# Which loads stand ahead of a data-dependent branch: mask alone, or mask behind weights and tables

## The chip, the cores and the metric

The kernel runs on one core of one Trainium2 chip. The metric is the device time of one execution in microseconds (us). A profile is one execution of the same program, recorded by the hardware profiler; its times are counted from the start of its span.

## The reference, cut to what matters

Eight sequences of 512 tokens with 256 channels pass through four layers: attention with one shared key/value head, a null key and a bias table; attention over the 16 heads inside each token; a mixture of eight experts with a shared expert; and a transformer layer whose feed-forward part is again a mixture. The layers behind the first matter here only as the work that follows. In the first layer:

```python
sim = jnp.einsum('bhid,bjd->bhij', q, k)          # k has the null key in front of the 512 tokens
sim = sim + bias                                  # null bias, then attn_bias
sim = jnp.where(causal_mask, neg, sim)
...                                               # and the padding mask: which keys may be seen
```

The padding mask has 8 x 512 bytes. `True` marks a key that may be attended to, and the inputs are made so that this holds only for the last positions of a sequence: `lenS = 512 - randint(0, 129)`, `mask = not (position < lenS)`. So the first 384 positions of every sequence are `False`. The kernel doesn't take this for granted: it looks at the mask, and branches.

## The kernel before, in words

One function, `tile_adaln_attn_ffn`, writes instructions for five engines; a layer beneath it (Tile) allocates buffers, sets the semaphores and orders the instructions of each engine's queue. An engine executes its queue strictly in order. Loads are issued by the sequencers of SP and ACT (`nc.sync.dma_start`, `nc.scalar.dma_start`), in the order of their queues.

**Ahead of the branch** (lines 63 to 408) stand constants made on POOL, the tables `cst`, `wr` and `br_bc`, a fill of the token table in DRAM (`ids<-none`), and the weights of the first layer (`wq`, `wo`, each 1 MB, `wkv`, and the small `gin`, `nvcol`, `nk_bc`, `nv_bc`, `nb_bc`) and of the second (`load_oh`: `awq`, `awd`, `awup`, `awout`, `gout`, `bdown`, `bq`, `bup`, `bout`). The first 384 columns of the mask are loaded as two rows of 1536 bytes in one partition each (`early_keys`, lines 363 to 368); VectorE takes the maximum of each row and of both, and `kept` is 1 if any early key is set. VectorE also makes `wn`, the null key times the query weights (four products and four sums, lines 395 to 408).

**The branch** (lines 1111 to 1115): every engine reads `kept` from memory into a register and compares it. If it is set, `any_keys` runs, the general attention; with these inputs it is skipped. The skipping path holds, for each engine, an addition to its semaphores of what the skipped instructions would have counted, and for SP the same for the eight counters of the transfers, each after a wait until the transfers ahead of the branch have landed.

**Behind the branch** `late_keys` (line 812) always runs: attention for the last 128 queries against the last 128 keys, and for all earlier tokens a constant row (`row`, from the null value and `wo`). In order:

- loads of the shared expert (`wtT`, `wgT`, `gT`, `swg`, `swu`, `swd`, lines 1239 to 1245, written ahead of the call), of tokens (`xp`, two sequences each), of the mask's tail (`m8`) and of four pieces of `bias`;
- the null value: `nvb` on VectorE, eight matmuls `pn<-wo,nvb`, then `row`;
- `prepare` for each of four pairs of sequences: normalise `xp`, transpose (`pt_x`), scale on ScalarE (`xT`), keys (`pk`), queries (`pq`), values and null scores (`pv`);
- scores (`pss`), softmax, output, for 16 units, and beside them (`beside`) `rest_load` and `rest_add` for the tokens that take the constant row, the second layer (`one_over_heads`, whose products `pr` run on POOL), and the first parts of the expert layer.

Everything later (three more groups of experts, the transformer layer, its mixture) follows in the order in which the queues were written. Eight counters (semaphores) are shared by all transfers of SP and ACT, in turn: a transfer can be issued only when the one that had its counter before has landed.

Of the kernel before, what the change touches and what calls it, by code (L numbers as in the profile page):

```python
# [9 lines left out]
F32 = mybir.dt.float32  # L10
U8 = mybir.dt.uint8
# [29 lines left out]
def tile_adaln_attn_ffn(ctx: ExitStack, tc: tile.TileContext, a: dict, out: bass.AP):  # L41
# [30 lines left out]
    nc.sync.dma_start(cst, a["c_misc"])  # L72
# [19 lines left out]
    def rows_of(vec, n=P):  # L92

        return vec.partition_broadcast(n)
# [19 lines left out]
    with nc.allow_non_contiguous_dma(reason="narrow rows"):  # L114
        nc.sync.dma_start(w_chosen, a["w_route"].rearrange("(k p) n -> p k n", p=P))
    br_bc = mid.tile([P, 12], F32, name="br_bc", tag="br_bc")
    nc.scalar.dma_start(br_bc, rows_of(a["b_route"]))
# [77 lines left out]
    none = ohp.tile([P, places // P], I32, name="none", tag="prod", bufs=4)  # L195
    nc.gpsimd.memset(none, B * S)
    nc.sync.dma_start(ids_d.rearrange("(p n) o -> p (n o)", p=P), none)
# [8 lines left out]
    def oh_load(name, shape, src, eng=None):  # L206
        t = ohp.tile(shape, F32, name=name, tag=name)
        (eng or nc.sync).dma_start(t, src)
        return t

    def oh_wload(name, src, cols):
        n = src.shape[0] // P
        return oh_load(name, [P, n, cols], src.rearrange("(k p) n -> p k n", p=P))

    OH_STEPS = 29
    oh_w = {}

    def load_oh():
        with nc.allow_non_contiguous_dma(reason="small vectors by partition"):
            oh_w["gout"] = oh_load("gout", [P, KD], cols_of(a["g_out"]), nc.scalar)  # L220
            oh_w["bdown"] = oh_load("bdown", [64, 1], a["bdown"].unsqueeze(1), nc.scalar)
        oh_w["awq"] = oh_wload("awq", a["aWq"], D)
        oh_w["awd"] = oh_wload("awd", a["aWdown"], 64)
        oh_w["awup"] = oh_load("awup", [64, 512], a["aWup"])
        oh_w["awout"] = oh_wload("awout", a["aWout"], D)
        oh_w["bq"] = oh_load("bq_bc", [P, D], rows_of(a["bq"]), nc.scalar)
        oh_w["bup"] = oh_load("bup_bc", [P, 2 * D], rows_of(a["bup"]), nc.scalar)
        oh_w["bout"] = oh_load("bout_bc", [P, D], rows_of(a["bout"]), nc.scalar)
# [134 lines left out]
    kept_i = aw.tile([1, 3], I32, name="kept", tag="kept")  # L363
    for u in range(2):
        early_keys = ohp.tile([1, B // 2, LAST * P], U8, name="early_keys", tag="prod", bufs=4)
        nc.sync.dma_start(early_keys, a["mask"][u * (B // 2) : (u + 1) * (B // 2), 0 : LAST * P].unsqueeze(0))
        nc.vector.tensor_reduce(kept_i[:, u : u + 1], early_keys, AX.XY, ALU.max)
    nc.vector.tensor_tensor(kept_i[:, 2:3], kept_i[:, 0:1], kept_i[:, 1:2], ALU.max)

    def load(name, shape, src, eng=None):  # L370
        t = aw.tile(shape, F32, name=name, tag=name)
        (eng or nc.sync).dma_start(t, src)
        return t

    def wload(name, src, cols):
        n = src.shape[0] // P
        return load(name, [P, n, cols], src.rearrange("(k p) n -> p k n", p=P))

    with nc.allow_non_contiguous_dma(reason="small vectors by partition"):
        gin = load("gin", [P, KD], cols_of(a["g_in"]), nc.scalar)  # L380
        nvcol = aw.tile([P, 1], F32, name="nvcol", tag="nvcol")
        for j in range(2):
            nc.scalar.dma_start(nvcol[j * 64 : (j + 1) * 64, :], a["cond"][1].unsqueeze(1))
    wq = wload("wq", a["Wq"], H * DH)
    wo = wload("wo", a["Wo"], D)
    wkv = wload("wkv", a["Wkv"], 2 * DH)
    nk_bc = load("nk_bc", [P, DH], rows_of(a["cond"][0]), nc.scalar)
    nv_bc = load("nv_bc", [P, DH], rows_of(a["cond"][1]), nc.scalar)
    nb_bc = load("nb_bc", [P, H], rows_of(a["null_bias"]), nc.scalar)
    load_oh()  # L390
    bias_v = a["attn_bias"].rearrange("(g hh j) q k -> g j q hh k", g=2, hh=4, j=2)


    wn = aw.tile([P, KD, 2, 2, 4], F32, name="wn", tag="wn")
    for k in range(KD):
        for g in range(2):
            pr = ohp.tile([P, 8, DH], F32, name="wn_pr", tag="prod", bufs=4)
            nc.vector.tensor_tensor(
                pr,
                wq[:, k, g * 512 : (g + 1) * 512].rearrange("p (h d) -> p h d", h=8),  # L400
                bc(nk_bc, 1, 8),
                ALU.mult,
            )
            nc.vector.tensor_reduce(
                wn[:, k, g].rearrange("p j hh -> p hh j"),
                pr.rearrange("p (hh j) d -> p hh j d", j=2),
                AX.X,
                ALU.add,
            )
# [8 lines left out]
    def any_keys():  # L418
        fill()
# [392 lines left out]
    def late_keys(first_group):  # L812
# [3 lines left out]
        with ExitStack() as ph:  # L816
# [14 lines left out]
            load_x(0)  # L831
            load_x(1)
# [5 lines left out]
            for g in range(2):  # L838
                for j in range(2):
                    nc.sync.dma_start(bias[:, g, j], bias_v[g, j, tail, :, tail])  # L840
                    nc.gpsimd.affine_select(
                        out=bias[:, g, j],
                        in_=bias[:, g, j],
                        pattern=[[0, 4], [-1, P]],
                        compare_op=ALU.is_ge,
                        fill=MASKED,
                        base=0,
                        channel_multiplier=1,
                    )
            ones = wp.tile([1, P], F32, name="ones", tag="ones")  # L850
# [6 lines left out]


            nvb = wp.tile([P, P], F32, name="nvb", tag="nvb")
            nc.vector.tensor_copy(nvb, nvcol.to_broadcast([P, P]))  # L860
            pn = ps_m.tile([P, D], F32, name="pn", tag="m")
            for c in range(8):
                nc.tensor.matmul(pn, nvb, wo[:, c, :], start=(c == 0), stop=(c == 7))
            null_row = wp.tile([1, D], F32, name="null_row", tag="null_row")
            nc.scalar.copy(null_row, pn[0:1, :])
            mv, rs = ln_stats(wk, [pn])
            row = wp.tile([P, D], F32, name="row", tag="row")
            nc.vector.tensor_scalar(row, pn, mv[:, 0, 0:1], rs[:, 0:1], ALU.subtract, ALU.mult)
# [212 lines left out]
            for _ in range(6):  # L1081
                next(prep)

# [27 lines left out]
    kept = nc.values_load(kept_i[:, 2:3], min_val=0, max_val=1)  # L1111
# [110 lines left out]
    with ExitStack() as ph:  # L1222
# [16 lines left out]
        with nc.allow_non_contiguous_dma(reason="small vectors by partition"):  # L1239
            wtT = wload("wtT", a["wtT"], E)  # L1240
            wgT = load("wgT", [64, E], a["wgT"], nc.scalar)
            gT = load("gT", [64, B], a["condT"], nc.scalar)
        swg = wload("swg", a["sw_gate"], 2 * P)
        swu = wload("swu", a["sw_up"], 2 * P)
        swd = wload("swd", a["sw_down"], D)
# [263 lines left out]
        late_keys(chain(route(0), route(1), mixture(0), mixed(0)))  # L1509
# [558 lines left out]
```

## Time and profile before

| What | Value |
|---|---|
| Times of three runs | 1849.16, 1856.75, 1860.49 us (median 1856.75) |
| Time of the profiled execution | 1837.18 us |
| Its span | 1835.1 us |
| Busy, share of the span | PE 85%, DVE 56%, ACT 32%, POOL 31% |
| Chain that ended last | PE 54%, DVE 16%, issue 14%, POOL 8%, DMA 4% |
| Mean granted TensorE clock | 0.899 |
| Bytes moved | 157.77 MB, mean 86 GB/s |
| First PE instruction | 27.1 us |

PE is the TensorE matmul stream, PEld its weight loads, DVE is VectorE, ACT is ScalarE, POOL is GpSimd, SP is SyncE; SPq and ACTq are the sequencers that issue transfers. The time of the profiled execution is 2.1 us above its span. A busy share is a mean over stages with different limits: the question of this document lies in the first 60 us, where PE is idle at first.

### The profile page before, as it was taken

What the parts mean: (1) busy time and instruction counts of PE and PEld (TensorE: products, weight loads), DVE (VectorE), ACT (ScalarE), POOL (GpSimd) and SP (SyncE); (2) the same over time, 40 slices, a digit from 0 to 9 for tenths busy, and PEclk for the clock granted to TensorE, in tenths of its full rate; (3) what the DMA queues carried; (4) which work ended last, traced back from release to release, by engine and by line L of the source; (5) the groups of instructions that cost most, each with busy time, mean ns of one, the idle gap of its engine ahead of it and who ended that gap; (6) DMA issues with size and microseconds to landing.
All of it is one profiled execution on the core that took longest, in us unless ns stands there. A gap on an engine that the chain in (4) does not pass through costs nothing.

```text
span 1835.1 us, 23467 instructions
## 1 busy us (share of the span) xinstructions
PE 1568.9 (85%) x7720; PEld 880.9 (48%) x7720; DVE 1031.2 (56%) x2709; ACT 583.9 (32%) x1281; POOL 561.3 (31%) x534
## 2 busy tenths in 40 slices
PE   2897888789897999998999899899899899639995
PEld 1664656543433554443554344454433333228884
DVE  3877554356673655555545656545756656225566
ACT  0433323202222332332353332344343343203331
POOL 2444351425445433103001302201201001147775
PEclk9897788867777989998999998999999999959998
DMA  5121236701114531002850102462100000046872
GB/s 167 39 83 35 83 110 201 199 26 38 32 54 144 165 98 38 19 1 92 190 157 30 36 7 66 109 182 67 37 1 7 13 1 14 4 154 212 238 222 66
DMA packets 189460, 157.77 MB, mean 86 GB/s; under 512 B 43214, under 2 KB 173774, under 8 KB 189329
## 3 DMA queue, kind: packets, MB, share of 16 engines
q1 hardware_dynamic: 147520, 109.10, 20.7%
q0 software_dynamic: 13056, 29.67, 5.1%
q10 hardware_dynamic: 28752, 17.41, 3.2%
q8 instruction: 63, 1.03, 0.3%
q14 instruction: 69, 0.56, 0.1%
HBM read 117.00 MB, written 44.21 MB: 88 GB/s over the span
## 4 chain that ended last, share of the span: by engine, by line
PE 54%; DVE 16%; issue 14%; POOL 8%; DMA 4%; ACT 1%; SPq 0%; POOLq 0%; ACTq 0%; DVEq 0%
PE pss L1613 12%; PE po_s L1660 6%; PE pg L1433 5%; PE pq_s L1565 3%; DVE nmz L1615 3%; PE pk_s L1571 3%; POOL pr L321 3%; POOL xs L1387 3%; PE px_s L1700 2%; PE py L1446 2%; PE pst L1637 2%; PE prs L1689 1%; PE pg L1483 1%; PE pv_s L1592 1%; DMA w_gu<-in_w_up_dram 1%
## 5 line engine op out<-in xcount | busy, mean ns | idle before, releaser
L1615 DVE TENSOR_REDUCE nmz<-pss 128x1 f32<-128x512 f32 x512 | 334.3, 685 | 224.2 <-PE pst L1637 188.7
L1638 ACT ACTIVATE pT_s<-pst 128x512 f32<-128x512 f32 x512 | 282.1, 595 | 448.7 <-PE pst L1637 443.3
L1613 PE MATMUL pss<-k_s,q_s 32*128 32x512 f32 x1024 | 360.7, 682 | 42.9 <-DVE nmz L1615 42.9
L1637 PE MATMUL pst<-q_s,k_s 32*128 32x512 f32 x1024 | 339.6, 670 | 4.5 <-DVE nmz L1615 3.6
L1613 PEld LDWEIGHTS pss<-k_s,q_s 32*128 32x128 f32 x1024 | 103.9, 192 | 229.0 <-DVE nmz L1615 104.9
L1660 PE MATMUL po_s<-pT_s,v 128*32 128x512 f32 x1024 | 165.6, 633 | 8.0 <-ACT pT_s L1638 8.0
L1278 POOL DMA_INDIRECT yg<-y,slot x64 | 66.4, 1038 | 301.7 <-DMA y<-y 170.7
L321 POOL TENSOR_TENSOR pr<-qk 128x512 f32<-128x512 f32 x72 | 89.8, 1282 | 103.5 <-DVE qk L299 67.2
L1433 PEld LDWEIGHTS pg<-xT,w_gu 128*128 128x128 f32 x768 | 95.6, 201 | 40.4 <-ACT xT L1424 17.1
L1433 PE MATMUL pg<-xT,w_gu 128*128 128x128 f32 x768 | 102.7, 289 | 13.3 <-ACT xT L1424 6.9
L321 POOL TENSOR_TENSOR pr<-at,v_h 128x512 f32<-128x512 f32 x72 | 90.5, 1288 | 67.1 <-DVE at L336 38.9
L1637 PEld LDWEIGHTS pst<-q_s,k_s 32*128 32x128 f32 x1024 | 96.8, 190 | 19.6 <-DVE nmz L1615 9.5
L1387 POOL DMA_INDIRECT xs<-x,slot x64 | 63.4, 991 | 126.1 <-DVE slot L1379 108.0
L1888 PE MATMUL ph<-xTj,w 128*128 128x256 f32 x368 | 85.7, 387 | 0.0
L1211 POOL DMA_INDIRECT ids<-token_id,pi x32 | 31.7, 992 | 174.0 <-DVE pi L1208 157.8
L1902 PE MATMUL py<-w,h_e 128*128 128x256 f32 x368 | 83.5, 380 | 1.4 <-issue 1.4
L1891 ACT ACTIVATE h_e<-ph,b 128x256 f32<-128x256 f32 x92 | 43.5, 473 | 108.8 <-PE ph L1888 105.1
L1888 PEld LDWEIGHTS ph<-xTj,w 128*128 128x128 f32 x368 | 71.5, 195 | 10.3 <-ACT xTj L1876 0.2
L1438 DVE TENSOR_TENSOR hh<-hh,pg 128x256 f32<-128x256 f32 x48 | 20.2, 420 | 97.0 <-ACT hh L1437 97.0
L1902 PEld LDWEIGHTS py<-w,h_e 128*128 128x128 f32 x368 | 68.2, 190 | 10.1 <-issue 1.8
L1565 PE MATMUL pq_s<-yT,wqp 128*128 128x512 f32 x128 | 68.7, 663 | 0.9 <-DVE hh L1439 0.7
L1712 POOL TENSOR_TENSOR e_rs<-e_ve,mhalf 128x4 f32<-128x4 f32 x8 | 8.9, 1108 | 192.9 <-DVE e_ve L1710 192.7
(298 smaller groups left out, 2604.2 us busy)
## 6 DMA issues: line engine op xcount, KB each, us to landing
w<-in_w_dram SPq DMA_DIRECT2D x46, 512.0 KB
w_gu<-in_w_gate_dram SPq DMA_DIRECT2D x96, 128.0 KB
w_gu<-in_w_up_dram SPq DMA_DIRECT2D x96, 128.0 KB
w_dn<-in_w_down_dram SPq DMA_DIRECT2D x96, 128.0 KB
xg<-xs SPq DMA_DIRECT2D x48, 256.0 KB
y<-y ACTq DMA_DIRECT2D x48, 256.0 KB
rows<-xr SPq DMA_DIRECT2D x8, 544.0 KB
x<-x SPq DMA_DIRECT2D x8, 512.0 KB
```

The lines of the kernel that those rows point to most:

```text
L321: nc.gpsimd.tensor_tensor(pr, x, y, ALU.mult)
L1278: nc.gpsimd.indirect_dma_start(out=yg[t][:, c, :], out_offset=None, in_=y1_d[grp], in_offset=bass.IndirectOffsetOnAxis(ap=yi[:, c, t : t + ...
L1387: sc_ = nc.gpsimd.indirect_dma_start(out=xs_d, out_offset=bass.IndirectOffsetOnAxis(ap=slot[:, bl, c, t : t + 1], axis=0), in_=xb[:, t, :] ...
L1433: nc.tensor.matmul(pg[:, c, u, :], w[:, u, c, k, :], xT[:, k, u, :], start=(k == 0), stop=(k == KD - 1))
L1565: nc.tensor.matmul(pq, wqp[:, k, gs], yT[:, k, :], start=(k == 0), stop=(k == KD - 1))
L1613: nc.tensor.matmul(pss, qs[n][r, t * P : (t + 1) * P], ks[n][r, :], start=True, stop=True)
L1615: yield lambda: nc.vector.tensor_reduce(nmz[n % 2].rearrange("p t (h r) -> p t h r", h=4)[:, t, h, HD : HD + 1], pss, AX.X, ALU.max, negat ...
L1637: nc.tensor.matmul(pst, ks[n][r, c * P : (c + 1) * P], qs[n][r, :], start=True, stop=True)
L1638: yield lambda: nc.scalar.activation(pT[:, u, :], pst, AF.Exp)
L1660: nc.tensor.matmul(pos[n][hd * 32 : hd * 32 + 32, :], v_sets[b % 3][:, c, (4 * g + hd) * VW : (4 * g + hd) * VW + 32], ws[hd // 2][:, hd % ...
L1888: nc.tensor.matmul(ph_, w1[:, k, c * P : (c + 1) * P], xT[:, k, :], start=(k == 0), stop=(k == KD - 1))
L1902: nc.tensor.matmul(py[:, u, :], h[:, c, u * P : (u + 1) * P], w2[:, c, :], start=(c == 0), stop=(c == 3))
```

## The change

Ahead of the branch only the mask's first 384 columns are read by name, now with one sequence to each of eight partitions; a maximum on VectorE, a 1 x 1 matmul that adds the eight, and a minimum with 1 give `kept`. The loads of weights and tables become functions that are called inside `late_keys` (and, for the first two layers' weights, inside `any_keys`): after the first tokens the weights `wkv`, `wq`, `wo`, then the second tokens, the bias, the second layer's weights, the shared expert's, the tables. `wn` and the null value are made between the steps of the first `prepare`.

```diff
-    nc.sync.dma_start(cst, a["c_misc"])
...
-        nc.sync.dma_start(w_chosen, a["w_route"].rearrange("(k p) n -> p k n", p=P))
-    nc.scalar.dma_start(br_bc, rows_of(a["b_route"]))
...
-    none = ohp.tile([P, places // P], I32, name="none", tag="prod", bufs=4)
-    nc.gpsimd.memset(none, B * S)
-    nc.sync.dma_start(ids_d.rearrange("(p n) o -> p (n o)", p=P), none)
...
+    def tables():
+        ...
+        nc.scalar.dma_start(br_bc, rows_of(a["b_route"]))
+        nc.sync.dma_start(cst, a["c_misc"])
+        none = ohp.tile([P, places // P], I32, name="none", tag="prod", bufs=4)
+        nc.gpsimd.memset(none, B * S)
+        nc.sync.dma_start(ids_d.rearrange("(p n) o -> p (n o)", p=P), none)
...
-    kept_i = aw.tile([1, 3], I32, name="kept", tag="kept")
-    for u in range(2):
-        early_keys = ohp.tile([1, B // 2, LAST * P], U8, name="early_keys", tag="prod", bufs=4)
-        nc.sync.dma_start(early_keys, a["mask"][u * (B // 2) : (u + 1) * (B // 2), 0 : LAST * P].unsqueeze(0))
-        nc.vector.tensor_reduce(kept_i[:, u : u + 1], early_keys, AX.XY, ALU.max)
-    nc.vector.tensor_tensor(kept_i[:, 2:3], kept_i[:, 0:1], kept_i[:, 1:2], ALU.max)
+    early = ohp.tile([B, LAST * P], U8, name="early_keys", tag="prod", bufs=4)
+    nc.sync.dma_start(early, a["mask"][:, 0 : LAST * P])
+    some = ohp.tile([B, 2], F32, name="some", tag="hm")
+    nc.vector.memset(some[:, 1:2], 1.0)
+    nc.vector.tensor_reduce(some[:, 0:1], early, AX.X, ALU.max)
+    kept_i = aw.tile([1, 1], I32, name="kept", tag="kept")
+    with tc.tile_pool(name="k_ps", bufs=1, space=PSUM) as kp:
+        pn = kp.tile([1, 1], F32, name="batches", tag="batches")
+        nc.tensor.matmul(pn, some[:, 0:1], some[:, 1:2], start=True, stop=True)
+        nc.vector.tensor_scalar(kept_i, pn, 1.0, None, ALU.min)
...
+    def load_weights():
+        with nc.allow_non_contiguous_dma(reason="small vectors by partition"):
+            nc.scalar.dma_start(gin, cols_of(a["g_in"]))
+            nc.scalar.dma_start(nk_bc, rows_of(a["cond"][0]))
+            for j in range(2):
+                nc.scalar.dma_start(nvcol[j * 64 : (j + 1) * 64, :], a["cond"][1].unsqueeze(1))
+        nc.sync.dma_start(wkv, a["Wkv"].rearrange("(k p) n -> p k n", p=P))
+        nc.sync.dma_start(wq, a["Wq"].rearrange("(k p) n -> p k n", p=P))
+        nc.sync.dma_start(wo, a["Wo"].rearrange("(k p) n -> p k n", p=P))
+        nc.scalar.dma_start(nv_bc, rows_of(a["cond"][1]))
+        nc.scalar.dma_start(nb_bc, rows_of(a["null_bias"]))
...
     def any_keys():
-        fill()
+        load_weights()
+        null_scores()
+        load_oh()
...
             load_x(0)
+            load_weights()
             load_x(1)
...
+            load_oh()
+            load_rest()
+            tables()
...
-            for _ in range(6):
+            for k in range(6):
                 next(prep)
+                if k == 0:
+                    null_scores()
+                elif k == 3:
+                    null_value()
```

`null_scores` holds the eight instructions for `wn`, `null_value` those for `pn` and `row`, `load_rest` the loads of the shared expert. Their instructions and their sizes are those of before; the buffers are now allocated ahead of the branch.

## The prediction

> **What bounds the kernel now.** I read the page first: TensorE (PE) is busy for 85% of the span, and the chain that ended last is 54% PE. So most of the run is a queue of matmuls, and a change in the loads counts only where that queue stands still. The timeline of the first 60 us shows where it does (start, length, engine, line, operation; in brackets the idle time before and what ended it):
>
> ```profile
> 15.85 3.40 DVE L367 TENSOR_REDUCE kept<-early_keys 1x1 int32<-1x1536 uint8 x2 [5.86 <-DMA early_keys<-in_mask_dram]
> 19.78 0.14 DVE L368 TENSOR_TENSOR kept<-kept 1x1 int32<-1x1 int32 x1
> 24.69 0.20 POOL L851 MEMSET ones<- 1x128 f32 x1 [21.88 <-PEq L1112]
> 26.19 0.38 SPq L1232 DMA_DIRECT2D wtT<-in_wtT_dram  x1
> 26.27 0.58 DVE L860 COPY nvb<-nvcol 128x128 f32<-128x128 f32 x1 [3.24 <-DVEq L1112]
> 39.77 1.22 PE L921 MATMUL pt_x<-ident,xp 128*128 128x128 f32 x4 [7.48 <-DMA xi<-in_x_dram]
> 48.63 0.63 PEld L968 LDWEIGHTS pv<-wkv,xT 128*128 128x128 f32 x4
> 57.16 6.17 POOL L321 TENSOR_TENSOR pr<-qk 128x512 f32<-128x512 f32 x5 [10.50 <-DVE qk L299]
> ```
>
> The branch's number is ready at 19.92 (19.78 + 0.14), and nothing of the attention is issued until 26.19, which I call B. Tokens come after that: the first transpose is at B + 13.6, the first value matmul `pv` at B + 22.4, the first products `pr` on POOL at B + 31.0. Why the number is late is told by the waits of SP's queue (who waited for what: total, times, longest):
>
> ```profile
> SPq L372 <- DMA nvcol<-in_cond_dram: 5.2, 1, 5.2
> SPq L1111 <- DVE kept L368: 3.4, 1, 3.4
> SPq L1112 <- SPq L1112: 2.8, 1, 2.8
> SPq L208 <- DMA wo<-in_Wo_dram: 2.0, 1, 2.0
> SPq L1232 <- DVEq L1112: 1.9, 1, 1.9
> ```
>
> The mask stands behind `wo`, and `wo` could only be issued when `nvcol`, which had its counter before, had landed. The last two L1112/L1232 rows are the branch itself: 2.8 us of jump, then 1.9 us until VectorE, which had `wn` to finish (until 23.03), had jumped too. Last the table of stretches (length, busy time and instructions of PE, PEld, DVE, ACT, POOL; clock, DMA share, GB/s):
>
> ```profile
> 0.00:20.00 20.00, 0.00 (x0) 0.00 (x0) 5.59 (x8) 0.00 (x0) 2.15 (x16) 1.00 0.69 193
> 26.00:41.00 15.00, 6.40 (x20) 4.72 (x20) 5.53 (x19) 1.65 (x2) 7.02 (x10) 0.87 0.75 229
> ```
>
> 3.9 MB move ahead of the branch and 3.4 MB behind it, in two bouts with a gap; tokens are in the second.
>
> **The change, part by part.**
>
> *The number.* The mask is now SP's first transfer, at 0.80. Nearest row: `gT`, a small load after a quiet stretch, was issued at 26.73 and used at 30.00, 3.3 us later. The first bytes of the whole run flow about 1.2 us after the first issue. Bounds 2.0 to 4.1 for the landing; I take 3.5. The maximum over 384 columns: 1.74 us for 1536 (3.40 / 2), so 0.44. The 1 x 1 matmul has no row; the narrowest, `pv` with 16 columns, are 0.57 for four, and with two hand-overs I give it 0.5. The minimum costs 0.14 as L368. Sum 4.6 (3.1 to 5.3).
>
> *The branch.* From 19.92 POOL needed 4.8 to its first instruction (24.69), SP 6.3 with the wait for VectorE in it. VectorE has nothing queued behind the number now, so I take 4.8: the new B, called S, is 4.6 + 4.8 = 9.4, 16.8 sooner (bounds 3.1 + 3.2, VectorE's own jump, and 5.3 + 6.3: 6.3 to 11.6). In the built program `wr`, `cst` and `br_bc` are still issued ahead of the branch, behind the mask, and SP's skipping path waits for them; their 150 KB should land before 8, under the jump: nothing. Only `none` and its write to `ids` go behind it; POOL's fill took 0.34 among memsets that nobody awaits.
>
> *The loads behind it.* SP's order is now `xp`, `wkv`, `wq`, `wo`, `xp`, four `bias`, the second layer's weights, the shared expert's, `ids`, `xp`, two `x_rest`, two `xi`; ACT's is `gin`, `nk_bc`, `nvcol` twice, `nv_bc`, `nb_bc`, `m8`, `gout`, `bdown`, `bq`, `bup`, `bout`, `wgT`, `gT`, and only then the table load and `xT`. Counters are still eight in turn, and the program's waits show whom each follows:
> - `wq`: ACT's `bq` followed it before and went at 8.13, so it took 5.9 after its issue ended (2.25). Now it has 384 KB ahead, 1.3 at 290 GB/s: S + 1.3 + 5.9 + 1.3 = S + 8.5.
> - `wo` follows the first `nvcol` (5.75 from issue at 1.71 to 7.46): S + 1.1 + 5.75 = S + 6.9, and lands 5.6 later (7.46 to 13.10, where `awq` could follow it): S + 12.5.
> - ACT: `bq` follows `wq`; five issues of 0.45 and the table load of 1.28 are ahead of `xT`, which was 7 us idle before: S + 8.5 + 2.3 + 1.3 = S + 12.1. No cost beside `wo`, but it is as late.
> - VectorE: `wn` was hidden ahead of the branch. It now waits for `wq`, 4 x (0.67 + 0.67) = 5.4, to S + 13.9, with `gb` (0.22, waiting for `gT`, ACT's last) and the key copy `kT` queued behind it.
>
> *PE.* Its queue is `pt_x`, one `pn`, `pk`, `pn`, half of `pq`, six `pn`, the rest of `pq`, `pv`. The first `pn` waits for `wo`, S + 12.5, and holds `pk` behind it. Then 0.65 + 1.97 (`pk`) and a 0.6 copy on VectorE that frees the bank: `pq` at S + 15.7, against B + 17.3. From there 5.5 (`pq`) and 3.9 (six of eight `pn`, 5.2 before) give S + 25.1. The 0.5 clock at 37 to 47 us lay under `pk` and `pq` before (0.34 each, against 0.26 at 54); it rose 7.1 us after PE restarted at 39.8, which here falls at S + 19.6 and saves 1.0 or so on the rest: `pv` at S + 24.1. That is 1.7 later after the branch than before, so the null value, hidden under the wait for tokens until now, costs part of the lead: 16.8 - 1.7 = 15.1 us.
>
> [...]
>
> *Transfers as a whole.* `pr` on POOL stands behind the two `xi` additions, and those behind the last transfer of the list: 7.2 MB from S. At the 290 GB/s of the fullest stretches that takes 25 us and 2 to start: S + 27, hidden, for `qk` is due at S + 32.6. At 229 (the row of 26 to 41, start included) it is S + 31.5, and with the additions (1.5), `ln_rs` (0.7), a scaling (0.4) and `qk` (0.4), 3.0 together, `pr` starts at S + 34.5: 1.9 late. At 193 (the row of 0 to 20) S + 37.4 and 7.8 late. I take 229, as the list is of that kind, and charge 1.1, since the scores of the other units go on beside POOL: 14.0 us gained. From `pr` on, all five queues stand in the order of before, with the same counters.
>
> *Sum.* 1837.2 (the profiled execution, span 1835.1 and 2.1 around it) - 14.0 = 1823.2. The runs shown have the median 1856.75, 19.5 above that execution; the edit touches nothing that differs between them, so I forecast 1842.5 as a median.
>
> **Rivals.**
>
> [...]
>
> *The transfers eat the lead:* at 193 GB/s, 15.1 - 7.8 = 7 gained, 1849.5. For it: in the first 20 us the waits on counters held the mean to 193, and the list has the same narrow loads (`nvcol`, `gin`) in its counters. Against: 37 transfers are eight deep, and most are 128 KB or more.
>
> *The branch isn't sooner,* or the engines wait for something that the number didn't gate: then S stays above 20 and the gain is under 5, 1852 to 1857. The 3.4 us that SP idled for the number speak against it.
>
> *Slower:* the counters make a chain. 37 transfers over 8 are 4.6 rounds; `xi` then lands at 4.6 times the round. At the longest landing seen, 5.75, that is S + 27. It decides from 9.7 us a round: S + 44.8, `pr` at 57.2, no gain; at 13.8 a round it costs 19 us, 1876. Nothing shows a round above 5.75, but loads of 4-byte elements queued behind 0.5 MB of broadcast rows weren't seen either.
>
> **How the numbers follow.** Forecast (gain of 9 to 17) 0.58; more 0.20; transfers or branch take most of it 0.15; slower 0.07. One per cent, about what a measurement of this kernel can tell from no change, is 18.6 us: the forecast lies inside it, and the runs of before spread over 11 us, so a part of the first two cases shows as faster by over 1%: 0.32. Within it 0.60, slower 0.08. The range goes from 1828 (18 gained, 1839, and the 11 of spread below it) to 1856 (7 gained, 1850, and half the spread above it); the forecast's own is 1834 to 1850.
>
> **What would show it.** Right: SP's first issue behind the branch near 9.4 (6 to 12), `wo` the last thing that PE waits for before `pk`, `pv` near 33.5, `pr` near 43, and the same distances as before from there on. Wrong: an S above 13; PE waiting on `gT` through VectorE, or on the key copy; `pr` waiting long for `xi`; or a lead of 14 us at 60 us that is gone at 400, which would make a later wait on a transfer the bound.

## The result and the profile after

The changed kernel takes 1844.4 us (median of 8 runs, 1839.55 to 1856.69) against 1855.26 for the kernel before on the same chip (8 runs, 1848.73 to 1860.49). The ratio is 0.9948, 95% interval 0.9923 to 0.9972: 9.6 us less, between 5.2 and 14.3. In two further groups of runs, both on one chip, the same program came to 0.9930 (0.9903 to 0.9958) and 0.9943 (0.9920 to 0.9966) of the kernel before. So the gain is about 11 us, inside the forecast's 9 to 17 and below its 14.0.

The profiled execution of the changed kernel took 1843.17 us, span 1841.5: longer than the one profiled execution of before (1837.18), which lay below every one of its eight timed runs. Single spans of this kernel vary by more than the change is worth; what can be compared between profiles is the first 60 us, and even there one execution does not stand for all (experiment 5). Timeline of the kernel after (start, length, engine, line, operation; in brackets idle time and what ended it):

```profile
3.14 0.15 DVE L377 TENSOR_SCALAR kept<-batches 1x1 int32<-1x1 f32 x1 [0.28 <-PE batches L376]
8.46 0.39 SPq L846 DMA_DIRECT2D xp<-in_x_dram  x1
10.36 0.40 SPq L404 DMA_DIRECT2D wq<-in_Wq_dram  x1
10.37 1.20 ACTq L402 DMA_DIRECT2D nvcol<-in_cond_dram  x2
18.88 0.33 ACTq L233 DMA_DIRECT2D bq_w<-in_bq_dram  x1
19.08 0.37 SPq L405 DMA_DIRECT2D wo<-in_Wo_dram  x1
19.28 0.23 DVE L885 COPY nvb<-nvcol 128x128 f32<-128x128 f32 x1 [6.06 <-DMA nvcol<-in_cond_dram]
20.09 1.09 PE L944 MATMUL pt_x<-ident,xp 128*128 128x128 f32 x4 [16.98 <-DVE xp L937]
27.59 0.50 PEld L888 LDWEIGHTS pn<-wo,nvb 128*128 128x128 f32 x2 [6.81 <-DMA wo<-in_Wo_dram]
28.74 1.97 PE L954 MATMUL pk<-xT,wkv 128*64 128x256 f32 x4
31.65 2.64 PE L970 MATMUL pq<-xT,wq 128*128 128x256 f32 x8
36.73 1.89 PE L970 MATMUL pq<-xT,wq 128*128 128x256 f32 x8
38.45 0.55 PE L991 MATMUL pv<-wkv,xT 128*128 128x64 f32 x4
47.37 6.27 POOL L326 TENSOR_TENSOR pr<-qk 128x512 f32<-128x512 f32 x5 [1.02 <-DVE qk L304]
```

The number is ready at 3.29, the end of the first row (19.92 before); SP's first issue behind the branch is at 8.46 (26.19 before). Of these 17.7 us, 10.4 are left at the first `pv` (38.45 against 48.85) and 9.8 at the first `pr` (47.37 against 57.16). The rest is lost between 11 and 27.6 us, where PE does four transposes and nothing else. What SP waited for in the first 60 us (who for what: total, times, longest):

```profile
SPq L405 <- DMA nvcol<-in_cond_dram: 8.3, 1, 8.3
SPq L858 <- DMA wo<-in_Wo_dram: 6.5, 1, 6.5
SPq L1139 <- SPq L1139: 3.5, 1, 3.5
SPq L1138 <- DVE kept L377: 1.1, 1, 1.1
```

The old wait for `nvcol` (5.2 before) is back, at 8.3, ahead of the same `wo`. PE waits for that `wo` at 27.59 (the weight load of `pn`, `PEld`), with `pk` and all that follows behind it. The 1.1 and 3.5 are the number and the jump. In the table of stretches the DMA engines between 9 and 20 us moved 140 GB/s and were busy for half of the time; behind `wo`'s issue they filled up (columns: length, busy time of PE, PEld, DVE, ACT, POOL; clock, DMA share, GB/s):

```profile
9.00:20.00 11.00, 0.00 (x0) 0.00 (x0) 2.12 (x8) 0.00 (x0) 4.76 (x6) 1.00 0.50 140
20.00:30.00 10.00, 3.50 (x9) 1.97 (x10) 5.93 (x11) 2.12 (x3) 0.64 (x1) 1.00 0.79 239
```

### The profile page after: what moved, and what is told of

The parts are those of the page before. It is cut to its first block, busy times and chain, and to the rows that moved or that the text cites. A ratio compares the mean times of both kernels' runs of the same rounds, so it can differ in the third digit from the quotient of the medians.

```text
span 1841.5 us, 23475 instructions
## 1 busy us (share of the span) xinstructions
PE 1576.4 (86%) x7722; PEld 884.6 (48%) x7722; DVE 1023.5 (56%) x2709; ACT 584.5 (32%) x1281; POOL 561.7 (31%) x534
## 4 chain that ended last, share of the span: by engine, by line
PE 68%; DVE 14%; issue 6%; POOL 5%; DMA 3%; another core or an unknown queue 1%; ACT 1%; ACTq 0%; SPq 0%; POOLq 0%; DVEq 0%
PE pss L1646 15%; PE po_s L1693 7%; PE pg L1466 5%; PE ph L1921 4%; PE pq_s L1598 4%; DVE nmz L1648 3%; PE py L1935 3%; PE pk_s L1604 3%; PE px_s L1733 3%; POOL pr L326 3%; PE pst L1670 2%; PE py L1479 2%; PE pv_s L1625 2%; PE pg L1516 2%; PE pu L1523 1%
## 5 line engine op out<-in xcount | busy, mean ns | idle before, releaser
L1646 PE MATMUL pss<-k_s,q_s 32*128 32x512 f32 x1024 | 367.8, 690 | 65.9 <-DVE nmz L1648 62.7
L1670 PE MATMUL pst<-q_s,k_s 32*128 32x512 f32 x1024 | 347.5, 681 | 5.8 <-DVE nmz L1648 3.6
L1466 PE MATMUL pg<-xT,w_gu 128*128 128x128 f32 x768 | 100.4, 285 | 10.7 <-ACT xT L1457 6.8
L1921 PEld LDWEIGHTS ph<-xTj,w 128*128 128x128 f32 x368 | 71.6, 195 | 10.4 <-ACT xTj L1909 0.2
L1935 PEld LDWEIGHTS py<-w,h_e 128*128 128x128 f32 x368 | 68.2, 190 | 10.1 <-issue 1.7
```

The costliest lines, as they stand in the source:

```text
L1466: nc.tensor.matmul(pg[:, c, u, :], w[:, u, c, k, :], xT[:, k, u, :], start=(k == 0), stop=(k == KD - 1))
L1646: nc.tensor.matmul(pss, qs[n][r, t * P : (t + 1) * P], ks[n][r, :], start=True, stop=True)
L1670: nc.tensor.matmul(pst, ks[n][r, c * P : (c + 1) * P], qs[n][r, :], start=True, stop=True)
L1921: nc.tensor.matmul(ph_, w1[:, k, c * P : (c + 1) * P], xT[:, k, :], start=(k == 0), stop=(k == KD - 1))
L1935: nc.tensor.matmul(py[:, u, :], h[:, c, u * P : (u + 1) * P], w2[:, c, :], start=(c == 0), stop=(c == 3))
```

## The experiments

"Gain" is always 1 - ratio times the median of the kernel before on the same chip, with its interval. "Lead" is how much sooner the first `pr` starts than in the kernel before (57.16).

**1. Is it the wait on `nvcol`?** The two `nvcol` loads alone go ahead of the branch (called kernel 1 below).

```diff
+    with nc.allow_non_contiguous_dma(reason="small vectors by partition"):
+        for j in range(2):
+            nc.scalar.dma_start(nvcol[j * 64 : (j + 1) * 64, :], a["cond"][1].unsqueeze(1))
+
     def load_weights():
...
-            for j in range(2):
-                nc.scalar.dma_start(nvcol[j * 64 : (j + 1) * 64, :], a["cond"][1].unsqueeze(1))
```

> Only the two `nvcol` loads (64 x 4 bytes each) move from behind the branch to ahead of it, on ACT's queue; `wo` then follows `nv_bc` on its counter. In the changed kernel `nvcol` was issued at 10.4 to 11.6 and landed 8.3 later with the DMA engines nearly empty, SP waited 8.3 for it, `wo` was issued at 19.1 and landed at 27.5, and the first `pn` with `pk` behind it began at 27.6. Theory A (the counter and the narrow load hold `wo`, and `wo` holds PE): `wo` is issued at 14 to 16, lands at 22 to 24, `pk` begins at 24 to 25 and `pv` at 34 to 35 instead of 38.2; the time falls by 3 to 4 us. Rival B (the DMA engines' throughput sets when `wo` lands): `wo` is issued sooner but still lands at 26 to 28, `pv` at 37 to 38, time the same within 1.5 us. Rival C (VectorE sets the start: `gb` waits for `gT`, the last of ACT's loads, and the key copy stands behind it): `wo` lands sooner, `pk` too, but `pq` waits for the key copy, and `pv` gains under 2 us.

Measured: 1818.01 us, ratio 0.9942 (0.9920 to 0.9964), gain 10.6 (6.6 to 14.6). Its timeline:

```profile
16.45 0.37 SPq L407 DMA_DIRECT2D wo<-in_Wo_dram  x1
22.37 1.97 PE L956 MATMUL pk<-xT,wkv 128*64 128x256 f32 x4 [1.73 <-ACT xT L952]
24.26 2.71 PEld L890 LDWEIGHTS pn<-wo,nvb 128*128 128x128 f32 x10 [0.76 <-DMA wo<-in_Wo_dram]
31.96 0.55 PE L993 MATMUL pv<-wkv,xT 128*128 128x64 f32 x4
40.64 5.04 POOL L326 TENSOR_TENSOR pr<-qk 128x512 f32<-128x512 f32 x4 [1.01 <-DVE qk L304]
```

`wo` landed by 24.3 instead of 27.6, and `pv` came 6.5 sooner than in the profile after. The DMA engines, nearly empty by the expectation, were busy for half of the time in the profile after (0.50 between 9 and 20 us). In these two executions the landing speaks against B (throughput), which wanted `wo` at 26 to 28, and against C, which wanted under 2 us at `pv`. It is not the last word: a second execution of this kernel (experiment 5) had `wo` issued at 18.22, landed at 26.19, and `pv` at 36.19. The time gained hardly more than the changed kernel's 9.6, and not the 3 to 4 us more that A wanted. Two questions followed: does the lead count, and is 38.45 typical of the changed kernel?

**2. Is it `pn` on PE?** No load is moved; the null value is written after the whole first `prepare`.

```diff
-                elif k == 3:
+                elif k == 5:
                     null_value()
```

> The null value (`nvb`, eight `pn`, `row`) is written after the last step of the first `prepare` instead of after its fourth, so on PE `pk`, `pq` and `pv` stand ahead of `pn` and don't wait for `wo`. No load is moved. Theory A (PE was held by `pn`'s wait for `wo`): `pk` begins when `xT` is ready, near 24 instead of 28.7, and `pv` at 30 to 32 instead of 38.2; the eight `pn` (about 5 us) come behind it, so `row` is as late as before or 1 us sooner, the scores `pss` begin at 36 to 37 instead of 40.2, and the time falls by 2 to 4 us. Rival C (VectorE's `wn`, `gb` waiting for `gT` at 27.6, and the key copy behind them set the start): `pk` is early but `pq` waits until the key copy is done at 28 to 29, `pv` at 34 to 35. Rival D (`row` and not the scores is what the following work waits for): `pv` is 6 us sooner and the products `pr` are not (47.4 within 1), and the time is the same within 1.5 us.

Measured: 1820.17 us, ratio 0.9964 (0.9938 to 0.9990), gain 6.6 (1.8 to 11.3).

```profile
20.83 1.97 PE L954 MATMUL pk<-xT,wkv 128*64 128x256 f32 x4 [2.46 <-ACT xT L950]
29.91 0.55 PE L991 MATMUL pv<-wkv,xT 128*128 128x64 f32 x4
31.61 3.70 PE L888 MATMUL pn<-wo,nvb 128*128 128x256 f32 x16
37.51 0.54 DVE L891 TENSOR_SCALAR row<-pn,ln_mv,ln_rs 128x256 f32<-128x256 f32 x1 [0.47 <-POOL ln_rs L88]
```

`pk` and `pv` left the wait for `wo` behind, as A said, and `pv` was the earliest of all; C's 34 to 35 is out. But `row`, at 37.51, was only 1.7 sooner than in the profile after (39.20), and `pr` began at 45.2: the second layer starts from `row`. The time did not fall by A's 2 to 4 us, and whether the null value is better early or late is not shown: 6.6 lies below the changed kernel's gains, but the intervals overlap. D's mechanism is there; its size is not settled, because `wo` itself was issued at 13.7 here and not at 19.1.

**3. Which half of the change brings the gain?** The first layer's loads are put back ahead of the branch, behind the mask, with the new way to form the number (weights ahead); in a second kernel the loads of `load_oh` and `tables` too (all ahead).

```diff
+    load_weights()
     def null_scores():
...
             load_x(0)
-            load_weights()
             load_x(1)
```

> The loads of the first layer's weights (`wkv`, `wq`, `wo` and the narrow `gin`, `nk_bc`, `nvcol`, `nv_bc`, `nb_bc`) are issued ahead of the branch again, behind the mask; everything else stays as in the changed kernel. Theory A (what counts is when `wo` lands, and the DMA engines were empty from 0 to 9 us): `wo` is issued near 8, lands at 14 to 15, and SP's part of the branch, which waits for all transfers ahead, ends at 15 to 17; tokens land 3.5 to 5 us behind that, the first transpose is at 20 to 22, nothing waits for `wo` any more, `pv` is at 31 to 33, and the time is 4 to 6 us below the changed kernel. Rival E (only an early first issue behind the branch counts, as the kernel's change supposes): the first issue is 7 to 8 later than 8.4 and `pv` is later than 38.2 by some of that, so the time is 2 to 6 us above the changed kernel.

> All loads of weights and tables stand ahead of the branch as in the kernel before, but behind the mask, and the new way to form `kept` is kept. This splits the change in two: the mask's place and form alone, without the loads behind the branch. Theory F (before, the number gated the branch, 19.9; the landings would gate it only a little sooner): SP can't leave the branch until the loads ahead of it have landed, so its first issue is at 17 to 20 against 26.2 before and 8.4 after, and `pv`, with all weights there, 22 us behind it or less: 38 to 42 against 48.6 and 38.2. The time is 6 to 11 us below the kernel before, so the mask's place brings most of the gain and the place of the loads little or nothing. Rival G (the loads' place brings the gain): first issue at 23 or later, `pv` at 45 or later, time within 4 us of the kernel before.

Measured: weights ahead 1822.7 us, ratio 0.9955 (0.9930 to 0.9981), gain 8.2 (3.5 to 12.8), first issue behind the branch at 15.90, lead 9.1. All ahead: 1829.16 us, ratio 0.9993 (0.9974 to 1.0012), gain 1.3 (-2.2 to 4.8), first issue at 24.56, lead 4.6. With all loads ahead the number was ready at 3.31, and still VectorE left the branch at 24.4 and SP at 24.6: the landings gate it as firmly as the number did (SP issued the last load ahead at 19.57, after a wait of 4.6 for `wo`). F's 17 to 20 is refuted, and so is its claim that the mask's place brings most of the gain; G's time holds, though not its `pv` at 45 (43.3). Moving the mask without the loads is worth 1.3 us, and 4.8 at most by its interval.

With the weights ahead, A missed in the time (8.2 gained is not 4 to 6 more than the changed kernel's 9.6) and E in the mechanism (`pv` at 36.7, not behind 38.2, though experiment 5 has the changed kernel's `pv` at 32.45 too): `wo` had landed before the branch, but `pt_x` came only at 26.56 instead of 20 to 22. The timeline shows a queue that nobody had on the list:

```profile
18.98 0.43 DVE L83 BATCH_NORM_STATS2 ln_st<-xp 128x6 f32<-128x256 f32 x1 [1.28 <-DMA xp<-in_x_dram]
24.53 0.64 POOL L859 TENSOR_SCALAR_AFFINE_SELECT bias<-bias 128x512 f32<-128x512 f32 x1 [2.80 <-DMA wgT<-in_wgT_dram]
25.13 0.72 POOL L88 TENSOR_TENSOR ln_rs<-ln_ve,mhalf 128x2 f32<-128x2 f32 x1
26.56 1.09 PE L944 MATMUL pt_x<-ident,xp 128*128 128x128 f32 x4 [23.47 <-DVE xp L937]
```

The tokens were there at 18.98, and `ln_rs` stood on POOL behind a piece of `bias` that had waited 2.80 (the row puts this wait down to the landing of `wgT`). When the landings come in another order, an engine's queue, which was written for the old one, can find a new instruction to stand behind.

**4. Does a microsecond of the branch count? And how steady is a profile?** Three kernels on one chip: the changed one and the one before, unchanged; and the changed one with 16 useless sums on VectorE, on which the number waits.

```diff
-    some = ohp.tile([B, 2], F32, name="some", tag="hm")
...
+    some = ohp.tile([P, 9], F32, name="some", tag="hm")
+    spin = ohp.tile([P, 8, DH], F32, name="spin", tag="prod", bufs=4)
+    nc.vector.memset(spin, 1.0 / DH)
+    for _ in range(16):
+        nc.vector.tensor_reduce(some[:, 1:9], spin, AX.X, ALU.add)
...
-        nc.tensor.matmul(pn, some[:, 0:1], some[:, 1:2], start=True, stop=True)
+        nc.tensor.matmul(pn, some[0:B, 0:1], some[0:B, 1:2], start=True, stop=True)
```

> The changed kernel once more, unchanged, on the chip of this group, so that the others can be set against it and not only against the kernel before. In the first group the gain in time was some 4 to 5 us smaller than the lead of the first products `pr` in each kernel (lead 16.6, 12.0, 9.1, 4.6; gain 11 to 12, 6.6 to 9, 6 to 8, 0 to 1). Theory H (something behind the front takes a fixed 4 to 5 us from every kernel with the loads or the mask moved): with `pr` at 47 (lead 9.8) the gain here is 4 to 6 us. Rival I (a lead counts in full, and the first group's kernels differ from their leads by the clock's chance only): 9 to 11 us.

> The kernel before, unchanged, for a second profile, on the chip of this group. Theory J (when TensorE's clock is halved follows from the work and comes again in every execution): the stretches at half clock lie at the same places of the span as in the first profile (10.2 us of them at 47.7, 20.5 at 153.5, 20.5 at 215), and the distances from `pr` to the first `xg` transpose (226 us) and on to the end are the same within 3 us. Rival K (they fall by chance): they lie elsewhere, and the distance from `pr` to `xg` differs by more than 5 us.

> The changed kernel with 16 useless sums of 512 columns on VectorE (0.68 us each in this case's profiles, some 11 to 12 us together) ahead of the branch's number; the number, the branch and all loads behind it are the same, only later. Theory M (a microsecond of the branch is a microsecond of the end): the number is ready at 12.5 to 14 instead of 3.3, the first issue behind the branch is at 17.5 to 19 instead of 8.4, all that follows keeps its distances, and the time rises by 9 to 11 us against the changed kernel on the same chip, to that of the kernel before. Rival N (later stages give back or take a part of any lead): the front moves as much, but the time by less than 6 us.

Measured: after 1823.54 us, ratio 0.9930, gain 12.8 (7.7 to 17.8), lead 10.6. Before again: 1832.65, ratio 0.9997 (0.9972 to 1.0022). The late number: 1832.78, ratio 0.9991 (0.9973 to 1.0009), gain 1.7 (-1.7 to 5.0); number at 13.79, first issue at 18.81, 10.35 later, and 9.2 us longer than the changed kernel on the same chip. M's 9 to 11 holds for the time: the two ratios' intervals don't overlap (0.9973 against 0.9958), so the delay costs time, though they don't exclude N's less than 6. H's gain of 4 to 6 us is refuted for the changed kernel.

But in the late kernel `pr` was only 4.3 later than in the profile after, although everything started 10.35 later: in that execution `wo` was issued 5.9 behind the first issue, not 10.6. So the front isn't the same in every execution, and M's "all that follows keeps its distances" failed. Theory J, that the clock's halvings come again at the same places, held only in part (the expectation counts its places 10.7 us later than from the start of the span, which is used here). By the clock's records the second profile of before has the 10.2 us at 36.7 (37.0 in the first) and 20.5 at 204.0 (204.2), but 23.9 at 139.1 instead of 20.5 at 142.8, and 20.5 at 227.8 where the first had 3.4 at 238.4 and 6.8 at 248.6; from `pr` to the first `xg` transpose it took 229.5 against 226.1, between J's 3 us and K's 5.

**5. The front varies from execution to execution.** A third profile of the changed kernel, beside kernel 1 again:

> The changed kernel, unchanged, on one chip with the two kernels below, so that they can be set against it directly. Expected 8 to 13 us below the kernel before, as in the two groups so far (ratios 0.9948 and 0.9930).

> The kernel with only `nvcol` moved ahead, again, beside the changed kernel. Its first products `pr` were at 40.6 against 46.5 to 47.4. Theory M (a lead in `pr` counts in full): 5 to 7 us below the changed kernel. Rival N (the stages up to 285 us, in which the first group's profile lost 6.5 of it, take it back each time): within 2.5 us of the changed kernel.

Measured: after 1825.1 us, ratio 0.9943, gain 10.5 (6.2 to 14.7); kernel 1 again 1819.8 us, ratio 0.9925 (0.9900 to 0.9950), gain 13.8 (9.2 to 18.4): 5.3 below the changed kernel as M said, but the two intervals overlap, so N is not excluded, and this profile of kernel 1 had `pv` at 36.19 and not at 31.96, `pr` at 44.9 and not at 40.6. In the changed kernel `pr` was at 41.7 and not at 47.4, without any edit. The two kernels' fronts overlap (`pv` at 31.96 and 36.19 against 38.45, 37.82 and 32.45), so single profiles cannot tell them apart. Its timeline:

```profile
9.24 2.07 ACTq L402 DMA_DIRECT2D nvcol<-in_cond_dram  x2
10.76 0.40 SPq L404 DMA_DIRECT2D wq<-in_Wq_dram  x1
12.75 0.37 SPq L405 DMA_DIRECT2D wo<-in_Wo_dram  x1
16.59 0.33 ACTq L233 DMA_DIRECT2D bq_w<-in_bq_dram  x1
16.67 0.23 DVE L885 COPY nvb<-nvcol 128x128 f32<-128x128 f32 x1 [3.49 <-DMA nvcol<-in_cond_dram]
21.46 1.22 PE L888 MATMUL pn<-wo,nvb 128*128 128x256 f32 x2 [2.89 <-DMA wo<-in_Wo_dram]
32.45 0.55 PE L991 MATMUL pv<-wkv,xT 128*128 128x64 f32 x4
```

Read it against the profile after. There `wq` was issued at 10.36 and the first `nvcol` at 10.37; here `nvcol` at 9.24 and `wq` at 10.76. `wo`'s issue shows when the first `nvcol` has landed, `bq`'s when `wq` has, `nvb` when both `nvcol` have. Five executions with this order of loads, all in us:

| | `nvcol` issued | `wq` issued | first `nvcol` landed | `wq` landed | both `nvcol` landed |
|---|---|---|---|---|---|
| after, first profile | 10.37 | 10.36 | 19.08 | 18.88 | 19.28 |
| after, second | 10.51 | 10.51 | 19.27 | 19.07 | 19.48 |
| after, third | 9.24 | 10.76 | 12.75 | 16.59 | 16.67 |
| `pn` last (2) | 9.50 | 9.49 | 13.71 | 16.25 | 16.48 |
| late number (4) | 19.53 | 19.81 | 24.69 | 27.91 | 27.66 |

The second `nvcol`, whose issue ended behind that of the megabyte of `wq` each time, lands within 0.1 to 0.4 us of it each time. The first one, where it was issued clearly ahead, lands 3.5 to 5.2 behind its issue and `wq` later; where the two were issued within 0.01 it went with `wq` twice and ahead of it once. So 256 bytes take 8.7 us in the first two rows, in which they report 0.20 behind `wq`. What goes with it: ACT's `nk_bc` issue just ahead takes 1.36 and 1.55 in these two, 0.43, 0.72 and 0.54 in the other three. Why, no run here tells. Nor is it shown that the order of the two issues is the whole difference: `gout`, which follows `nk_bc` on its counter, could go only at 16.25 and 16.41 in the first two profiles of the changed kernel and went at 13.89 in the third, so a load issued ahead of both was late as well.

**6. Clearing the front.** Three kernels. In the first, narrow loads ahead, the eight loads `gin`, `nvcol` (two), `gout`, `bdown`, `nk_bc`, `nv_bc` and `nb_bc` stand ahead of the branch, in this way:

```diff
+        nc.scalar.dma_start(gin, cols_of(a["g_in"]))
...
+    nc.scalar.dma_start(nb_bc, rows_of(a["null_bias"]))
     def load_weights():
...
-            nc.scalar.dma_start(gin, cols_of(a["g_in"]))
```

The second, ACT free, is kernel 1 with `gout`, `bdown`, `bq`, `bup` and `bout` issued by SP, in this way:

```diff
-            nc.scalar.dma_start(oh_w[name], rows_of(a[name]))
+            nc.sync.dma_start(oh_w[name], rows_of(a[name]))
...
```

The third, tail first, is the second with the mask's tail as ACT's second load behind the branch (only `gin` stays ahead of it):

```diff
+            m8 = ohp.tile([65, B, P], U8, name="m8", tag="prod", bufs=4)
+            nc.scalar.dma_start(m8[64:65], a["mask"][:, tail].unsqueeze(0))
             load_x(0)
             load_weights()
             load_x(1)
...
```

> All loads of a few bytes a row (`gin`, `nvcol`, `gout`, `bdown`, `nk_bc`, `nv_bc`, `nb_bc`) are issued ahead of the branch; behind it `wo` follows the first tokens on its counter. Theory A (narrow loads in the eight counters hold the wide ones, and SP stands still for them): SP's first issue stays at 8 to 9.5, `wo` is issued at 11 to 14 (16.5 with only `nvcol` moved, 19.1 in the changed kernel) and lands before 21, the first transpose is at 14 to 17, `pv` at 27 to 31 (32.0 and 38.2), and the time is 4 to 7 us below the changed kernel on the same chip. Rival B (the sum of transfers sets the pace): `wo` and `xT` are no sooner than with `nvcol` alone (24 and 21.8), `pv` 32 or later. Rival L (the narrow loads ahead delay the branch instead): SP's first issue at 11 or later, and the gain is gone.

> As the one before, and the five narrow or broadcast loads of the second layer (`gout`, `bdown`, `bq`, `bup`, `bout`) are issued by SP instead of ACT, so that ACT is free for `xT` as soon as `gT` is issued, and doesn't wait for `wq` by way of `bout`. Theory A (issuing queues that wait on counters hold the front): ACT's last issue is before 16, `xT` begins at 17 to 20 instead of 21.8 (and 23.2 in the changed kernel), `wo` is issued at 12 to 16, `pv` is at 28 to 31. Theory M: 7 to 10 us below the changed kernel, if the two `xi`, which now follow the broadcast rows on SP, don't hold `pr`. Rival N: within 3 us of it. Rival O (`pr` waits for `xi`, which comes later in SP's queue): `pv` is early, `pr` at 41 or later, no better than the kernel with only `nvcol` moved.

> As the kernel that freed ACT, and the mask's tail `m8` is loaded as ACT's second transfer behind the branch instead of its sixth, so that VectorE's `kT<-m` doesn't stand waiting (3.3 us there, 2.8 with only `nvcol` moved) between the two halves of the first tokens. Theory A: `kT<-m` is done before 14, the four transposes `pt_x` before 17, `xT` begins at 16 to 18 (22.1 there), then `wo`, issued at 12 to 14 and landed at 18 to 21, is the last thing that PE waits for, `pv` at 27 to 30, `pr` at 36 to 39 (40.7 there, 57 before). Theory M (a lead in `pr` counts, less the 1 to 5 us by which all kernels of this case have fallen short of it): 13 to 19 us below the kernel before, the best of all. Rival P (gains of the front end at 10 to 12 us, whatever the lead): ratio to the kernel before 0.993 to 0.995. Rival Q (narrow loads land late wherever they stand): `kT<-m` is as late as before, `pv` at 32.

Measured. Narrow loads ahead: 1823.07 us, ratio 0.9941 (0.9917 to 0.9966), gain 10.8, `wo` issued at 13.84, but SP's first issue came at 11.09 (ACT still had loads to issue until 7.4), `kT<-m` waited 2.76, and `pv` was at 33.07. L held in part, and B's numbers came; whether with B's cause is open, for `wo` was used only at 25.00, 11.2 behind its issue. The time was 0.5 us below the changed kernel in the same group, not A's 4 to 7. ACT free: 1824.6 us, 0.9938 (0.9912 to 0.9963), gain 11.4; `wo` at 12.46, ACT's last issue done at 14.0, but `xT` at 22.14 all the same, since VectorE's `kT<-m` waited 3.26 for the mask's tail between the two halves of the tokens; `pr` at 40.73 waited for `qk` and not for `xi`, so O is out. Its time was 0.5 us below the changed kernel in the same group, as N said, and not M's 7 to 10. Tail first: 1819.87 us, 0.9919 (0.9894 to 0.9945), gain 14.9 (10.1 to 19.4), the largest of all.

```profile
12.04 0.37 SPq L407 DMA_DIRECT2D wo<-in_Wo_dram  x1
13.01 0.99 DVE L856 TENSOR_SCALAR kT<-m 1x1024 f32<-1x1024 uint8 x1
16.50 1.09 PE L946 MATMUL pt_x<-ident,xp 128*128 128x128 f32 x4 [13.28 <-DVE xp L939]
18.95 0.84 ACT L952 ACTIVATE xT<-pt_x,gin 128x256 f32<-128x256 f32 x2
31.30 0.55 PE L993 MATMUL pv<-wkv,xT 128*128 128x64 f32 x4
39.62 4.92 POOL L326 TENSOR_TENSOR pr<-qk 128x512 f32<-128x512 f32 x4 [6.17 <-DVE qk L304]
```

`kT<-m` no longer waits, the transposes run together at 16.50, PE's work begins at 19.5. So Q is out. `pn` waited for `wo` until 22.15, 10.1 behind its issue, and `pv` at 31.3 and `pr` at 39.6 just miss what was expected (27 to 30 and 36 to 39). M's 13 to 19 came. This version is below the kernel before by more than any other; against the changed kernel, which wasn't on its chip, the ratios' intervals overlap, and the interval reaches into P's 0.993 to 0.995 as well.

**Lead and gain together.** One profile's lead of `pr` and the kernel's gain in time, each gain within some 4 or 5 us:

| Kernel | Lead, us | Gain, us |
|---|---|---|
| all ahead | 4.6 | 1.3 |
| late number | 5.5 | 1.7 |
| weights ahead | 9.1 | 8.2 |
| after, three groups | 9.8, 10.6, 15.4 | 9.6, 12.8, 10.5 |
| `pn` last | 11.9 | 6.6 |
| kernel 1, two groups | 16.5, 12.3 | 10.6, 13.8 |
| narrow loads ahead | 15.6 | 10.8 |
| ACT free | 16.4 | 11.4 |
| tail first | 17.5 | 14.9 |

The two kernels with the smallest leads gain least, and on average a gain is 2.8 less than its lead. Among the leads of 9 and more the order is not kept: 12.3 went with 13.8, 15.6 with 10.8. The interval of every one of these reaches into 10 to 12 (`pn` last ends at 11.3, tail first begins at 10.1), so a gain that ends there whatever the lead (P) is not excluded; nor is it settled where the 2.8 go, for a lead belongs to one execution and a gain to many.

## Why the prediction was right, point by point

*The number and the branch* held. `kept` came at 3.29 instead of 4.6, because the mask was in use at 2.33 (3.5 was taken; 2.0 to 4.1 were the bounds). The branch from number to SP took 5.2 (4.8 taken). S is 8.3 to 8.5 instead of 9.4. Experiment 3 adds what the prediction had not separated: the number alone doesn't release the branch, the loads ahead hold it as well. With the number early and all loads ahead the first issue came 1.6 us sooner than before, with the first layer's loads ahead 10.3, with both parts of the change 17.7. The loads moved without the new number were not tried.

*`wo` holds PE* held as a mechanism; it is the row that says so (the weight load of `pn` waits for `wo` until 27.59, `pk` is behind it), and so do the second and third profile (27.82 and 21.45). Its size was off, at two terms. The landing of `nvcol` was taken at 5.75 from the row of before and came to 8.7 in two of three executions, where it reports 0.2 behind `wq`; the prediction had `wq` and `nvcol` as two terms side by side (S + 8.5 and S + 6.9), and there both came at S + 10.4 to S + 10.9. And `wo`'s own 5.6 was 8.5 (19.08 to 27.59), with the second `xp` and a bias piece issued right behind it; in the third execution it was 8.7 (12.75 to 21.46). Together `wo` landed at S + 19.1 instead of S + 12.5, and `pv` came at 38.45 instead of 33.5: the 15.1 us of lead were 10.4. In the third execution, in which `nvcol` was ahead, `pv` came at 32.45, S + 24.2 against the S + 24.1 that the prediction wrote. That is in part luck: `nvcol` took 3.5 instead of 5.75 and `wo` 8.7 instead of 5.6, and the two errors cancel.

*A term was missing:* `nvb` stands on VectorE ahead of the tokens' scaling, so `nvcol` held the transposes too (20.09, right behind 19.28). It cost nothing beside `wo`.

*The pace of the matmuls*, in the prediction the clock's rise, rose sooner than booked in this profile, but not at a fixed time. The saving of 1.0 was booked from the rise 7.1 us after PE's restart. Measured: `pk` took 0.49 a matmul, the first eight `pq` 0.33 and the last eight 0.24. The pace went from 0.43 to 0.22 a matmul at 32.9, 5.3 us after PE's restart; in the second execution 3.9, in the third 5.8, with the late number 4.1, with `pn` last 8.4. All these have gaps in them. The `pn` of the kernel before have none, 16 matmuls in a row, and there the two profiles differ:

```profile
27.12 5.18 PE L863 MATMUL pn<-wo,nvb 128*128 128x256 f32 x16 [27.12 <-DVE nvb L860]
27.39 6.60 PE L863 MATMUL pn<-wo,nvb 128*128 128x256 f32 x16 [27.39 <-DVE nvb L860]
```

The pace doubled about 3.0 us after the first matmul in one and 5.9 in the other, so no single time could have been booked. The slower pace stands under 1.00 in the clock column of the table of stretches.

*Transfers as a whole* didn't bind `pr`. The 1.1 us charged for them was not needed: POOL's first `xi` addition was at 42.04, `pr` at 47.37 waited 1.02 for `qk` alone. From `pv` to `pr` it took 8.9 instead of 8.3, by the row for `qk` and not for transfers. The sign of being wrong that looks furthest, a lead that is gone at 400 us, did not come: the first row maximum `nmz` of the transformer layer starts at 387.9 and 391.6 in the two profiles of before and at 377.2, 385.8 and 378.2 in the three of the changed kernel, 9.4 sooner on average. That the first profile after is the longer one all the same is made behind this place; by what is open.

*The rivals.* "More", with its 0.20, and the lower end of the range stand on a gain of 18 that no run shows: the three groups of the changed kernel gained 9.6, 12.8 and 10.5, and `wo` held PE until 27.59, 21.45 at the earliest. "Transfers eat the lead" with its gain of 7 lies in the first measurement's interval, and half of its reason came: a narrow load in the counters held the mean to 140 GB/s between 9 and 20 us. The other half, `pr` late behind the last transfer, did not. "Slower": the first `nvcol` took 8.7 where 5.75 was the longest landing seen, but such rounds didn't add up to a chain: 4.6 of them would have put `xi` at S + 40, and it was used at 42.04, S + 33.6. The forecast of 1842.5 sits 1.9 from the median though the lead at `pv` was 4.7 too large in the first profile: the runs spread over 17 us, some executions have `nvcol` in front and the full lead, and a gain of 14 was not told from one of 9.6. Part of this nearness is luck: the kernel before came out at 1855.26, 1.5 below the median that the forecast started from.

## What to carry to other kernels

The branch of this kernel is released by the latest of the number and everything that must have landed ahead of it; moving the number alone gained 1.3 us, moving the loads as well 11. When loads go behind such a branch, list for every engine what it stands behind in the new order of landings: here a 256-byte load, 8.7 us from issue to landing, held a weight, a copy and a queue of matmuls, and clearing three such waits one after the other (narrow load ahead, ACT's queue free, mask's tail first) went with a gain of 14.9, which the intervals don't separate from 11. And profile such a start more than once: three executions of one program had their first value matmul at 38.5, 37.8 and 32.5.

## What the runs showed of the hardware

- A narrow load whose issue ended behind that of a wide one, from another queue, landed within 0.1 to 0.4 us of the wide one in five executions of five (table in experiment 5).
- An instruction stood behind a waiting one of its engine: `pk` behind `pn` on PE until 28.74 in the profile after, though its `xT` was done at 24.06 (with `pn` written last it began at 20.83, as `xT` came), and `ln_rs` on POOL behind a piece of `bias` that had waited 2.80 us (experiment 3).
- From the number to SP's first issue behind the branch it took 4.9 to 5.2 us in every kernel whose loads were not in the way, 3.2 to 3.5 of them put down to SP's own jump.
- The clock column of the table of stretches shows 1.00 where matmuls run at half their later pace (27.6 to 32.9 in the profile after, `pq` at 0.43 us a matmul against 0.22 later). The clock records of this trace begin at 33.17, so the column does not tell the pace there. The same 16 `pn` without a gap took 5.18 and 6.60 us in the two profiles of the kernel before.
- In the clock records of the first profile of before, every stretch at half (0.50) but the one that the end of the run cuts is 3.4 us long or a multiple of it (6.8, 10.2, 13.7, 20.5 and longer). In the second profile the stretches begin at about the same places as far as 100 us (36.7, 74.2 and 84.5 against 37.0, 74.5 and 84.8) and at partly other places behind that.
